# Two layer norms of a four-layer graph network without a mean: centred weights, a mean square on ScalarE, a mask on ScalarE, and new planner shares

## The chip, the cores and the metric

The kernel runs on one NeuronCore of a Trainium2 chip. The core has five engines with queues of their own, each of which works in order: TensorE (PE, with its weight loads as PEld), VectorE (DVE), ScalarE (ACT), GpSimd (POOL) and SyncE (SP, which only issues DMAs here). The metric is the time of one execution on the device, in microseconds (us), as the median of several runs; one further execution is profiled. Faster, the same and slower are relative to the kernel before.

## The reference

There are 32 graphs of 512 nodes with 64 features. Each graph has a sparse weighted adjacency matrix. Four layers follow each other, and each adds its result to its input and normalizes over the 64 features:

```python
def _layernorm(x, axis=-1, eps=1e-5):
    m = jnp.mean(x, axis=axis, keepdims=True)
    v = jnp.var(x, axis=axis, keepdims=True)
    return (x - m) / jnp.sqrt(v + eps)
...
    x = _layernorm(x + _L0_gnn_ref(x, adj), axis=-1)
    x = _layernorm(x + _L1_gnn_ref(x, adj, L1_gnn_weight, L1_gnn_bias), axis=-1)
    x = _layernorm(x + _L2_gnn_ref(x, adj, L2_gnn_att_W, L2_gnn_att_b), axis=-1)
    x = _layernorm(x + _L3_gnn_ref(x, adj, nodemask, L3_gnn_W1, L3_gnn_b1, L3_gnn_W2, L3_gnn_b2), axis=-1)
```

Layer 0 averages the neighbours. Layer 1 is a Chebyshev filter of four orders, whose results are multiplied by a weight of 256 x 64 and get a bias. Layer 2 is an attention in hyperbolic space over all pairs of nodes. Layer 3 takes weighted quantiles over each node's neighbours (which needs a sort) and feeds them through two dense products, `h = relu(out @ W1 + b1)`, `y = (h @ W2 + b2) * mask`. The norm after layer 1 and the norm after layer 3 are those that the change touches.

## The kernel before

Nodes lie on the 128 partitions, four tiles (T = 4) to a graph. Per graph the work is cut into lanes. *front* loads the adjacency matrix in four pieces, transposes it on PE, does layers 0 and 1 and normalizes into FL (lines 966 to 1054). *pairs* does the pairwise work of layer 2 in tiles of 128x512 and 128x640, and *tail* its end and norm (1056 to 1238). *graph* computes the neighbour lists and ranks (862 to 964). *gather* builds one-hot matrices and lets PE place the neighbours' features in slots (1240 to 1302). *sort* runs a sorting network on DVE over the tile SB, graph by graph, and *head* one over SH for two graphs together (1338 to 1393). *head* then calls `finish` and `dense` (1414 to 1459): ranked results go to DRAM, come back by an indirect DMA, and pass the two dense products, the mask, the residual add, the last norm and the output DMA. The last two graphs skip the way through DRAM (`spots`, the tiles "ends"). *check* tests limits; a dense fallback (1573 to 1709) is in the program but isn't taken with these inputs.

The order of the instructions is not the order of the code. The class `Order` (240 to 462) records every operation of all 32 graphs with its engine, an assumed cost and its dependencies. `due` (332) gives each a due time: the graph's number plus a share between the two numbers of its lane in `STAGES` (1506), times a period of 80. `issue` (357) then lets each engine take, of the operations that it assumes to be ready, the one due first. A handover between engines counts as the tail of the first operation plus `HOP` plus `LATE` (355). On PE, `STAY` (395) favours the weight shape in use. Where the plan leaves PE idle, small filler matmuls go in (`stay_active`, 1542 to 1545). The engines then run their queues in that fixed order and wait by semaphores.

A layer norm (796 to 811) is, on DVE, four `bn_stats` and four `bn_aggr` (one for each tile of nodes), an add of epsilon; on POOL a power of -0.5 (793); on DVE again the offset -mean times that; on ACT four activations with a scale and a bias for each node. It is called at 1008 (layer 0), 1047 (layer 1, which reads PE's result in PSUM), 1234 (layer 2) and 1458 (layer 3). In `front` the variance is used once more for the squared length of the normalized row (1051). The mask before the last norm is one DVE product of 128x256 (1456). `square` (826) and `scaled` (813) exist already and are used in the tail: four ACT squares that also give their sum, and four ACT copies with a scale for each node.

Of the kernel before, what the change touches and what calls it, by code (L numbers as in the profile page):

```python
# [15 lines left out]
OP = mybir.AluOpType  # L16
# [223 lines left out]
class Order:  # L240
# [3 lines left out]

    ENGINES = ("PE", "DVE", "ACT", "POOL", "SP")
    HOP = 0.05
    LATE = 0.124
    STAY = 39.7

    def __init__(self, nc, tc):  # L250
        self.nc, self.tc = nc, tc
# [214 lines left out]
def tile_adj_resnorm(ctx: ExitStack, tc: tile.TileContext, x, adj, nodemask, w1k, b1k, att_w, att_b,  # L466
# [221 lines left out]
    def rows(src, n, name, m, home=const):  # L688
        t = home.tile([m, n], F32, name=name)
        nc.scalar.dma_start(t, bass.AP(tensor=src.tensor, offset=src.offset, ap=[[0, m], [1, n]]))  # L690
        return t

    def parts3(src, name):

        rem, n = src, src.shape[-1]
        full = first.tile([3, n], F32, name=name + "s")
        part3 = first.tile([3, n], BF16, name=name + "p")
        out = const.tile([P, n], BF16, name=name)
        nc.vector.memset(out, 0.0)
        for k in range(3):  # L700
            nc.vector.tensor_copy(part3, rem)
            if k:
                stt(full, part3, identf[:3, k:k + 1], full, op0=OP.mult, op1=OP.add)
            else:
                ts(full, part3, identf[:3, 0:1], None, op0=OP.mult)
            tt(rem, rem, part3, op=OP.subtract)
        nc.vector.tensor_copy(out[:3, :], full)
        return out
# [1 line left out]
    b1f = first.tile([3, D + 2], F32, name="b1f")  # L710
    nc.scalar.dma_start(b1f[:, :D], bass.AP(tensor=b1k.tensor, offset=b1k.offset, ap=[[0, 3], [1, D]]))
    attb = rows(att_b, 1, "attb", P)
    bias2 = parts3(rows(b2, D, "b2f", 3, first), "bias2")
    meanf = first.tile([D, D], F32, name="meanf")
    nc.vector.memset(meanf, 1.0 / D)
    attw = const.tile([D, 2], F32, name="attw")
# [17 lines left out]
    nc.scalar.dma_start(b1s, b1.rearrange("(h u) -> h u", u=1))  # L734
    w2s = const.tile([HID, D], F32, name="w2s")
    nc.scalar.dma_start(w2s, w2)

    nmask = const.tile([P, T, B], F32, name="nmask")
    with tc.tile_pool(name="ps_0", bufs=1, space=PSUM) as ps:
        nm8 = first.tile([B, N], U8, name="nm8")  # L740
        nc.scalar.dma_start(nm8, nodemask)
        nmf = first.tile([B, N], F32, name="nmf")
        nc.vector.tensor_copy(nmf, nm8)
        pm = ps.tile([P, 512], F32, name="pm")
        for t in range(T):
            nc.tensor.transpose(pm[:, t * B:(t + 1) * B], nmf[:, t * P:(t + 1) * P], identf[:B, :B])
        nc.vector.tensor_copy(nmask, pm[:, :T * B].rearrange("p (t b) -> p t b", b=B))


        pw = ps.tile([P, 512], F32, name="pw")  # L750
        nc.tensor.matmul(pw[:D, :2], meanf, attw, start=True, stop=True)
        tt(attw, attw, pw[:D, :2], op=OP.subtract)
        wkT = first.tile([D, P], F32, name="wkT")
        for u in range(KO * D // P):
            pw = ps.tile([P, 512], F32, name="pw")
            nc.tensor.transpose(pw[:D, :P], wk[:, u, :D], identf)
            nc.vector.tensor_copy(wkT, pw[:D, :P])
            pw = ps.tile([P, 512], F32, name="pw")
            nc.tensor.matmul(pw[:, :2], wkT, attw, start=True, stop=True)
            nc.vector.tensor_copy(wk[:, u, D:], pw[:, :2])  # L760
        pw = ps.tile([P, 512], F32, name="pw")
        nc.tensor.matmul(pw[:3, :2], b1c.to_broadcast([D, 3]), attw, start=True, stop=True)
        nc.vector.tensor_copy(b1f[:, D:], pw[:3, :2])
    bias1 = parts3(b1f, "bias1")
    xs = dram.tile([B, N, D], F32, name="xs")
    ranked = [dram.tile([N, D], F32, name=f"ranked{b}") for b in range(B)]
# [7 lines left out]
    def bc(a, n=D):  # L774

        return a.unsqueeze(2).to_broadcast([P, T, n])
# [19 lines left out]
    def layernorm(dst, z):  # L796

        st = seq.tile(pools["small"], [P, T, nc.vector.BN_STATS_DIM], F32, "st", 2)
        mv = seq.tile(pools["small"], [P, T, nc.vector.BN_AGGR_DIM], F32, "mv", 2)
        for t in range(T):  # L800
            bn_stats(st[:, t, :], z[:, t, :])
        for t in range(T):
            bn_aggr(mv[:, t, :], st[:, t, :])
        var = col("var")
        ts(var, mv[:, :, 1], EPS, None, op0=OP.add)
        rs = rsqrt(var, "rs")
        off = col("off")
        stt(off, mv[:, :, 0], -1.0, rs, op0=OP.mult, op1=OP.mult)
        for t in range(T):
            act(dst[:, t, :], z[:, t, :], AF.Identity, bias=off[:, t:t + 1], scale=rs[:, t:t + 1])  # L810
        return mv[:, :, 1], rs

    def scaled(out, a, s):

# [151 lines left out]
    def front(b, res):  # L966

        A, xa = load(b)
        mid = pools["mid"]
        AT = transposed(A)  # L970
        res["AT"] = AT

        def amul(rhs, n):

            pt = bank()[:, :T * n].rearrange("p (t n) -> p t n", n=n)
            for t in range(T):
                for j in range(T):
                    mm(pt[:, t, :], AT[:, j, t * P:(t + 1) * P], rhs[:, j, :],
                                     start=(j == 0), stop=(j == T - 1))
            return pt  # L980

        def amul_split(y):

            half = N // 2
            pt = bank()[:, :half]
            for j in range(T):
                for h in range(2):
                    mm(pt[h * D:(h + 1) * D, :], y[:, j, :], AT[:, j, h * half:(h + 1) * half], start=(j == 0), stop=(j == T - 1),
                       pair=True)
            uT = seq.tile(mid, [P, half], F32, "uT", 1)  # L990
            act(uT, pt, AF.Copy)
            pt = bank()[:, :T * D]
            for u in range(2):
                tr(pt[:, u * P:(u + 1) * P], uT[:, u * P:(u + 1) * P], identf)
            return pt.rearrange("p (u h n) -> p h u n", h=2, n=D)


        pt = amul(xa, D + 1)
        deg = col("deg")
        cp(deg, pt[:, :, D])  # L1000
        dc = col("dc")
        ts(dc, deg, 1.0, None, op0=OP.max)
        recip(dc, dc)
        z = wide("z")
        tt(z, pt[:, :, :D], bc(dc), op=OP.mult)
        tt(z, z, xa[:, :, :D], op=OP.add)
        R = seq.tile(mid, [P, T, KO * D], F32, "R", 1)
        layernorm(R[:, :, :D], z)


        dm = col("dm")
        ts(dm, deg, 2e-35, None, op0=OP.max)
        dsc = rsqrt(dm, "dsc")
        pos = col("pos")
        ts(pos, deg, 0.0, None, op0=OP.is_gt)
        tt(dsc, dsc, pos, op=OP.mult)
        g = col("g")
        ts(g, deg, 0.0, None, op0=OP.not_equal)
        for k in range(1, KO):
            prev = R[:, :, (k - 1) * D:k * D]  # L1020
            y = wide("y")
            tt(y, prev, bc(dsc), op=OP.mult)
            pt = amul_split(y)
            q = wide("q", "y")
            tt(q.rearrange("p (h u) n -> p h u n", h=2), pt, dsc.rearrange("p (h u) -> p h u", h=2).unsqueeze(3).to_broadcast([P, 2, 2, D]),
               op=OP.mult)
            cur = R[:, :, k * D:(k + 1) * D]
            if k == 1:
                pg = wide("pg", "z")
                tt(pg, prev, bc(g), op=OP.mult)  # L1030
                prev = pg
            tt(cur, prev, q, op=OP.subtract)
        RT = seq.tile(mid, [P, KO * D // P, N], F32, "RT", 1)
        for u in range(KO * D // P):
            pt = bank()
            for t in range(T):
                tr(pt[:, t * P:(t + 1) * P], R[:, t, u * P:(u + 1) * P], identf)
            act(RT[:, u, :], pt, AF.Copy)
        pt = bank()[:, :T * (D + 2)].rearrange("p (t n) -> p t n", n=D + 2)
        nu = KO * D // P  # L1040
        for t in range(T):
            mm(pt[:, t, :], onesb, bias1, start=True, stop=False)
            for u in range(nu):
                mm(pt[:, t, :], RT[:, u, t * P:(t + 1) * P], wk[:, u, :], start=False, stop=(u == nu - 1))

        FL = FLS[:, b % 2]
        var, rs = layernorm(FL[:, :, :D], pt[:, :, :D])
        tt(FL[:, :, D + 2:D + 7:4], pt[:, :, D:], bc(rs, 2), op=OP.mult)

        w2 = col("w2")  # L1050
        stt(w2, var, float(D), rs, op0=OP.mult, op1=OP.mult)
        tt(FL[:, :, D:D + 34:33], bc(w2, 2), bc(rs, 2), op=OP.mult)
        ts(FL[:, :, D + 3:D + 36:32], bc(FL[:, :, D], 2), -1.0, 1.0, op0=OP.mult, op1=OP.add)
        res["FL"] = FL
# [381 lines left out]
    def dense(po, x3T, x3, dst, nm, home=None):  # L1436
# [16 lines left out]
            mm(py[:, t, :], onesb, bias2, start=True, stop=False)  # L1453
            mm(py[:, t, :], hT[:, t * P:(t + 1) * P], w2s, start=False, stop=True)
        z = home[1] if home else wide("zo")
        tt(z, py, bc(nm), op=OP.mult)
        tt(z, z, x3, op=OP.add)
        layernorm(z, z)
        dma(dst.rearrange("o (t p) d -> p (o t) d", p=P), z)

    flag = const.tile([1, 1], I32, name="flag")
# [13 lines left out]
    def within_bounds():  # L1475
# [17 lines left out]
        for i, op in enumerate((OP.is_gt, OP.is_lt)):  # L1493
# [9 lines left out]

    STAGES = {"front": (-0.6, -0.25), "pairs": (0.89, 1.46), "tail": (0.89, 1.49), "graph": (0.9, 1.59),
              "gather": (2.75, 2.76), "sort": (4.36, 5), "head": (4.74, 5.84), "ends": (2.6, 3.56), "check": (3.14, 3.68)}

    nc.scalar.preload_act_table_set("natural_log_exp_and_others")
    with ExitStack() as fast:  # L1510
# [285 lines left out]
```

## Time and profile before

| | before |
|---|---|
| timed runs, median of 3 | 2387.07 us (2385.55 to 2387.8) |
| profiled execution | 2391.38 us |
| its span, first to last instruction | 2389.5 us |
| granted PE clock, mean | 0.993 |
| PE fillers (lines 1544, 1545) | 761, busy 102.9 us |
| DVE group front_st<-front_bank (785) | 128, busy 29.1 us, mean 228 ns |
| DVE group head_st<-head_zo (785) | 124, busy 20.5 us, mean 209 ns |
| DVE group front_mv<-front_st (788) | 256, busy 33.8 us, mean 162 ns |
| DVE group head_zo<-head_bank,nmask (510) | 31, busy 12.8 us, mean 414 ns |
| ACT group tail_junk<-tail_u (546), and its accumulator reads | 128, busy 32.2 us, mean 252 ns; 128, busy 24.3 us, mean 190 ns |
| ACT group tail_v<-FLS,tail_s (546) | 128, busy 34.1 us, mean 337 ns |

Busy times of a group are the union of its instructions; neighbouring instructions of an engine overlap at their ends, so an instruction's duration is longer than the distance to the next one's start. A line number in a row may be that of a helper: 510 is a DVE operation on two tensors, 514 one with scalars, 517 one with a scalar and two tensors, 546 every ACT activation, 565 every matmul, 570 every transpose, 578 the indirect DMA, 793 the power on POOL. The prefix of a tile's name is its lane. "Idle before" is the time that the engine stood still just before an instruction, and after the arrow is what ended it.

### The profile page before, as it was taken

The numbers are of one execution on the slowest core, as the hardware profiler recorded it, in microseconds if no ns is written. First come the engines' busy times: TensorE is split into PE (matmuls) and PEld (weight loads), VectorE is DVE, ScalarE is ACT, GpSimd is POOL, SyncE is SP. The second block draws the span as 40 slices with busy tenths as digits, with TensorE's granted clock in tenths as the row PEclk, the third lists the DMA queues.
The fourth block names the chain that finished last, engine by engine and source line by source line (L and its number), as shares of the span: only waits on it lengthen the run. The fifth ranks groups of instructions, "written<-read, shape, count | busy, mean of one in ns | idle before, by whom it ended". The sixth has DMA issues, their size and how long they took to land.

```text
span 2389.5 us, 54114 instructions
## 1 busy us (share of the span) xinstructions
PE 2211.2 (93%) x19059; PEld 1559.4 (65%) x19059; DVE 2220.7 (93%) x7670; ACT 1862.6 (78%) x4602; POOL 1122.4 (47%) x2255
## 2 busy tenths in 40 slices
PE   7999999999999999999999999999999999999887
PEld 5666666666666666766666666666666666666555
DVE  4668899999999999999999999999999999999996
ACT  5788878787878877887887788787788878778841
POOL 1243345545454555545555544554545455454430
PEclk9999999999999999999999999999999999999999
DMA  1100001101001110100101010010101000000000
GB/s 42 34 28 23 15 15 31 27 23 35 19 19 27 28 29 24 32 17 23 28 27 31 23 32 17 23 28 26 32 23 32 16 25 26 21 21 4 15 15 11
DMA packets 131716, 57.75 MB, mean 24 GB/s; under 512 B 56140, under 2 KB 129516, under 8 KB 131436
## 3 DMA queue, kind: packets, MB, share of 16 engines
q1 hardware_dynamic: 126432, 50.09, 7.7%
q0 software_dynamic: 3840, 3.94, 0.9%
q8 instruction: 152, 2.49, 0.4%
q14 instruction: 128, 1.05, 0.1%
q10 hardware_dynamic: 1164, 0.18, 0.0%
HBM read 41.86 MB, written 12.32 MB: 23 GB/s over the span
## 4 chain that ended last, share of the span: by engine, by line
DVE 67%; PE 19%; ACT 7%; issue 4%; POOL 2%; DMA 0%; ACTq 0%; POOLq 0%; DVEq 0%
DVE SB L510 17%; PE front_bank L565 7%; DVE SH L510 7%; DVE gather_oh L514 7%; PE gather_bank L565 3%; DVE pairs_Wt L517 3%; PE graph_bank L565 3%; DVE pairs_L L517 3%; DVE pairs_Q L510 2%; PE pairs_bank L565 2%; DVE sort_prod L510 2%; DVE pairs_RW L510 2%; DVE pairs_EX L517 2%; DVE front_st L785 2%; DVE PRS L510 2%
## 5 line engine op out<-in xcount | busy, mean ns | idle before, releaser
L510 DVE TENSOR_TENSOR SB<-SB 128x92 f32<-128x92 f32 (+12 forms) x1312 | 548.3, 446 | 8.3
L565 PE MATMUL gather_bank<-gather_oh,tail_x3h 128*64 128x448 f16 (+5 forms) x5376 | 470.1, 317 | 2.8 <-ACT SB L546 2.3
L565 PEld LDWEIGHTS <-tail_x3h 128*64 128x64 bf16 x5376 | 293.2, 110 | 142.5 <-issue 43.0
L565 PE MATMUL pairs_bank<-pairs_FT 67*128 67x512 f32 (+7 forms) x768 | 309.9, 513 | 35.2 <-ACT pairs_FT L546 13.1
L510 DVE TENSOR_TENSOR SH<-SH 128x288 f32<-128x288 f32 (+18 forms) x880 | 269.2, 340 | 6.4
L514 DVE TENSOR_SCALAR gather_oh<-graph_slot 128x256 f16<-128x256 f16 (+9 forms) x864 | 257.0, 340 | 9.5 <-PE gather_bank L565 9.5
L565 PE MATMUL front_bank<-front_AT,front_y 128*64 128x256 f32 x1536 | 188.3, 383 | 23.7 <-DVE front_y L510 20.9
L565 PEld LDWEIGHTS pairs_bank<-pairs_FT 67*128 67x128 f32 (+1 forms) x768 | 127.5, 191 | 115.4 <-ACT pairs_EX L546 24.6
L578 POOL DMA_INDIRECT tail_x<-ranked,graph_spot x120 | 144.4, 1203 | 110.0 <-issue 68.9
L793 POOL TENSOR_TENSOR front_rs<-front_var,mhalf 128x4 f32<-128x4 f32 x64 | 91.4, 1428 | 204.2 <-DVE front_var L514 194.6
L565 PEld LDWEIGHTS front_bank<-front_AT,front_y 128*64 128x64 f32 x1536 | 118.5, 136 | 75.9 <-DVE front_y L510 29.2
L565 PEld LDWEIGHTS <-graph_nbT 128*128 128x128 f16 x1536 | 113.2, 97 | 62.0 <-issue 27.0
L565 PE MATMUL graph_bank<-graph_perm,graph_V 128*128 128x512 f16 x512 | 142.2, 379 | 7.3 <-ACT graph_VP L546 5.0
L565 PEld LDWEIGHTS pairs_bank<-FLS,pairs_Wt 128*128 128x128 f32 x1024 | 128.6, 191 | 22.4 <-DVE pairs_Wt L517 14.5
L565 PE MATMUL pairs_bank<-FLS,pairs_Wt 128*128 128x66 f32 x1024 | 130.7, 272 | 9.0 <-DVE pairs_Wt L517 7.3
L565 PEld LDWEIGHTS front_bank<-XA,front_AT 128*128 128x128 f32 x1024 | 127.8, 192 | 16.1 <-issue 6.3
L546 ACT ACTIVATE graph_V<-graph_bank 128x512 f16<-128x512 f32 x128 | 75.8, 592 | 74.4 <-PE graph_bank L565 74.3
L546 ACT ACTIVATE graph_slot<-graph_bank 128x512 f16<-128x512 f32 x128 | 75.6, 591 | 67.0 <-PE gather_bank L565 39.1
L565 PE MATMUL front_bank<-XA,front_AT 128*128 128x65 f32 x1024 | 124.3, 270 | 0.2 <-issue 0.2
L793 POOL TENSOR_TENSOR tail_rs<-tail_var,mhalf 128x4 f32<-128x4 f32 x32 | 40.0, 1251 | 162.0 <-DVE tail_var L514 86.3
L565 PEld LDWEIGHTS <-tabs 128*128 128x128 f16 x1296 | 78.3, 98 | 49.8 <-issue 32.0
L510 DVE TENSOR_TENSOR pairs_RW<-pairs_RW,pairs_EX 128x640 f32<-128x640 f32 x128 | 104.4, 816 | 6.7 <-ACT pairs_RW L546 6.7
(359 smaller groups left out, 6408.5 us busy)
## 6 DMA issues: line engine op xcount, KB each, us to landing
front_A<-in_adj_dram SPq DMA_DIRECT2D x128, 256.0 KB, 2.8
XA<-in_x_dram SPq DMA_DIRECT2D x32, 128.0 KB, 2.3
xs<-tail_x SPq DMA_DIRECT2D x32, 128.0 KB, 2.0
out_dram<-head_zo SPq DMA_DIRECT2D x31, 128.0 KB, 1.9
ranked<-sort_ap SPq DMA_DIRECT2D x30, 128.0 KB, 1.9
tail_x<-ranked,graph_spot POOLq DMA_INDIRECT x120, 2.5
out_dram<-tail_ends SPq DMA_DIRECT2D x1, 128.0 KB, 2.0
wk<-in_L_gnn_weight_dram ACTq DMA_DIRECT2D x1, 64.0 KB, 3.0
```

The costliest lines, as they stand in the source:

```text
L510: vec(lambda: nc.vector.tensor_tensor(out, a, b, op=op), out, [a, b])
L514: vec(lambda: nc.vector.tensor_scalar(out, a, s1, s2, op0=op0, **kw), out, [a], True, (s1, s2))
L517: vec(lambda: nc.vector.scalar_tensor_tensor(out, a, s, b, op0=op0, op1=op1), out, [a, b], False, (s,))
L546: 0.1, lambda: nc.scalar.activation(out, a, f, scale=scale, **kw), [out, accum_out], [a, after] + sc, table)
L565: return nc.tensor.matmul(out, w, a, start=start, stop=stop)
L578: seq.op("POOL", 1.15, 2.0, lambda: nc.gpsimd.indirect_dma_start(out, None, rows, bass.IndirectOffsetOnAxis(ap=at, axis=0)), [out], [at], ...
L785: vec(lambda: nc.vector.bn_stats(out, a), out, [a], reads=a)
L793: seq.op("POOL", 1.6, 0.5, lambda: nc.gpsimd.tensor_tensor(y, v, mhalf, op=OP.pow), [y], [v])
```

## The change

Subtracting from each row of a weight its mean over the 64 outputs makes every product of it have a mean of zero. For layer 1 the identity of the residual is already part of the weight (line 726), so the whole input of the norm is centred; the bias is centred too. For layer 3 the dense product is centred; the residual that is added to it is the output of the norm before, whose mean is zero, and the mask is one number for each node. So both norms leave out the mean: ACT takes the squares and their sum, DVE makes variance plus epsilon of it, POOL the power, ACT the product. The mask becomes four ACT copies with a scale. `LATE`, `STAY` and all of `STAGES` get new values.

```diff
-    LATE = 0.124
-    STAY = 39.7
+    LATE = 0.029
+    STAY = 31.6
...
+    def centred(a, n):
+
+        m = first.tile([a.shape[0], a.shape[1] if len(a.shape) > 2 else 1], F32, name=f"mean{n}")
+        for u in range(m.shape[1]):
+            row = a[:, u, :] if len(a.shape) > 2 else a
+            reduce(m[:, u:u + 1], row, OP.add)
+            ts(m[:, u:u + 1], m[:, u:u + 1], 1.0 / D, None, op0=OP.mult)
+            ts(row, row, m[:, u:u + 1], None, op0=OP.subtract)
+        return a
...
-    bias2 = parts3(rows(b2, D, "b2f", 3, first), "bias2")
+    bias2 = parts3(centred(rows(b2, D, "b2f", 3, first), 0), "bias2")
...
     nc.scalar.dma_start(w2s, w2)
+    centred(w2s, 1)
...
+    centred(wk[:, :, :D], 2)
+    centred(b1f[:, :D], 3)
     bias1 = parts3(b1f, "bias1")
...
+    def norm_centred(dst, z):
+
+        ss = square(z, "ss")
+        var = col("var")
+        ts(var, ss, 1.0 / D, EPS, op0=OP.mult, op1=OP.add)
+        rs = rsqrt(var, "rs")
+        scaled(dst, z, rs)
+        return ss, rs
...
-        var, rs = layernorm(FL[:, :, :D], pt[:, :, :D])
+        ss, rs = norm_centred(FL[:, :, :D], pt[:, :, :D])
...
-        stt(w2, var, float(D), rs, op0=OP.mult, op1=OP.mult)
+        tt(w2, ss, rs, op=OP.mult)
...
-        tt(z, py, bc(nm), op=OP.mult)
+        scaled(z, py, nm)
         tt(z, z, x3, op=OP.add)
-        layernorm(z, z)
+        norm_centred(z, z)
...
-    STAGES = {"front": (-0.6, -0.25), "pairs": (0.89, 1.46), "tail": (0.89, 1.49), "graph": (0.9, 1.59),
-              "gather": (2.75, 2.76), "sort": (4.36, 5), "head": (4.74, 5.84), "ends": (2.6, 3.56), "check": (3.14, 3.68)}
+    STAGES = {"front": (-0.46, -0.3), "pairs": (0.89, 1.21), "tail": (1.6, 2.5), "graph": (0.93, 1.24),
+              "gather": (2.63, 2.8), "sort": (3.87, 4.78), "head": (4.25, 5.37), "ends": (4.04, 4.45), "check": (1.75, 2.07)}
```

## The prediction

> **What bounds the kernel now.** I read the busy table first, then the same busy times cut into stretches of 280 us (four graphs), then the waits of VectorE (DVE), then the order of time on DVE and ScalarE (ACT).
>
> ```profile
> span 2389.5 us, 54114 instructions
> PE 2211.2 (93%) x19059; PEld 1559.4 (65%) x19059; DVE 2220.7 (93%) x7670; ACT 1862.6 (78%) x4602; POOL 1122.4 (47%) x2255
> ```
> ```profile
> core 0: us, PE busy (x) PEld busy (x) DVE busy (x) ACT busy (x) POOL busy (x), PEclk, DMA share, GB/s
> 760.00:1040.00 280.00, 262.94 (x2296) 185.96 (x2296) 273.79 (x946) 228.73 (x571) 143.87 (x275) 1.00 0.10 26
> 1040.00:1320.00 280.00, 262.95 (x2297) 185.91 (x2295) 273.77 (x946) 228.71 (x572) 143.85 (x275) 1.00 0.10 26
> 1320.00:1600.00 280.00, 262.95 (x2295) 185.84 (x2293) 273.80 (x945) 228.72 (x571) 143.89 (x275) 1.00 0.10 26
> ```
>
> The page gives PE and DVE 93% each and decides nothing. The stretches do: from about 140 us to 2360 us the work repeats (the same front matmul stands in the chain at 889.84, 1029.78 and 1169.71, so two graphs take 139.94 and one 69.97), and there DVE is busy 273.8 of 280, 97.8%. Per graph DVE is busy 68.45 and idle 1.55, PE 65.74 and 4.26, ACT 57.18 and 12.8. DVE sets the pace; the first 140 us (DVE busy 75.1) and the last 25 are ramps. The chain of waits agrees: DVE 67%, PE 19%.
>
> ```profile
> DVE front_st L785 <- PE front_bank L565: 16.0, 41, 0.8
> DVE pairs_RW L510 <- ACT pairs_RW L546: 4.1, 10, 0.4
> ```
>
> These are DVE's two largest waits between 480 and 1880 us, which is 20 graphs. Half of DVE's idle time (16.0/20 = 0.80 per graph) stands before the statistics of layer 1's last norm, which wait for one matmul group after the other.
>
> **What goes from DVE.** On a full queue an instruction costs the distance to the next one's start, less than its duration:
>
> ```profile
> 1043.58 0.41 DVE L510 TENSOR_TENSOR tail_v<-tail_v,tail_u 128x256 f32<-128x256 f32 x1
> 1043.92 0.34 DVE L514 TENSOR_SCALAR graph_v<-graph_v,graph_skip 128x512 f16<-128x512 f16 x1
> 1044.18 0.59 DVE L785 BATCH_NORM_STATS2 tail_st<-tail_v 128x6 f32<-128x64 f32 x4
> 1044.69 0.36 DVE L788 BATCH_NORM_AGGREGATE tail_mv<-tail_st 128x2 f32<-128x6 f32 x4
> 1044.97 0.32 DVE L514 TENSOR_SCALAR graph_v<-graph_v,graph_skip 128x512 f16<-128x512 f16 x1
> ...
> 1053.24 0.23 DVE L785 BATCH_NORM_STATS2 front_st<-front_bank 128x6 f32<-128x64 f32 x1
> 1053.39 0.21 DVE L514 TENSOR_SCALAR gather_oh<-graph_slot 128x256 f16<-128x256 f16 x1
> ```
>
> - Layer 1's norm: four statistics from PSUM at 0.15 (1053.24 to 1053.39), four aggregations at 0.10, the offset 0.07: 1.07. The new front_w costs 0.07 like the old.
> - The last norm: four statistics 0.51 (1044.18 to 1044.69), four aggregations 0.28, offset 0.07; the mask, 256 elements like tail_v, 0.34: 1.20.
>
> Together 2.27 per graph. The instruction order of the two programs, which I compared engine by engine, confirms the counts: 256 statistics, 256 aggregations, 64 offsets and 32 masks fewer, nothing added but 15 small instructions at the start. The other end of the price is the whole durations of the groups (29.1 + 16.9 + 4.9 and 21.1 + 11.4 + 4.8 + 13.2 = 101.4 us, 3.17 per graph); I take 2.27, because the queue is full, and keep 3.17 for the low end.
>
> **The wait of 0.80** moves to ACT, which now reads the front's bank group by group. DVE gets three new handovers per graph instead: front_var and head_var wait for ACT's sums, and the residual add for ACT's mask. Bounds: nothing, as tail_u shows (2.8 us in all after ACT's scaled copies, 0.09 per graph), to 0.4 each, the longest single pairs_RW wait, 1.2 per graph. I take 0.15 each, the size of the rows tail_v (4.6 us in all) and graph_v (4.5): 0.45.
>
> **What ACT gets.**
>
> ```profile
> 1078.13 1.06 ACT L546 ACTIVATE tail_v<-FLS,tail_s 128x64 f32<-128x64 f32 x4
> ```
>
> Squares with a sum already run in the tail: the tile's ACT busy time is 5.47 us in four graphs, 1.37 for four squares with their accumulator reads. Two such norms: 2.74. The mask as four scaled copies: 1.06 (the row above). The two last activations lose their bias operand and fall from 1.29 and about 1.45 to 1.06 each: -0.62. Net +3.18, so ACT goes from 57.2 to 60.4 in a step of about 67.4: 90%. What hides it is ACT's 12.8 us of idle time per graph, of which 2.4 is waiting for PE before graph_V; if that cover were gone, ACT would set a step of 69.97 + 3.18. PE's order before and after differs in fillers: 761 become 554, at 102.9/761 = 0.135 each 28 us of PE, all but 0.54 per graph of the old ones in the ramps.
>
> One rule speaks against the move of the mask: the Trainium skill, "ScalarE: Activation LUTs", section Rules for kernel authors, sends multiplications to VectorE. By its roughly 0.3 us per activation and 0.83 ns per element, four copies of 64 would be an estimated 1.4 us against the 1.06 in the row. The trace grants the rule that ACT's form is dearer (1.06 against 0.34), and on a kernel bound by ACT the sum by it would be a loss. Here the engine that is full is DVE, and the row decides.
>
> **Moved by the order.** The new shares (STAGES), LATE and STAY give other priorities, so all queues are reordered; the DMAs on SP and the work on POOL keep their counts. Pricing the DVE instructions of both orders with the rows above, between a graph's layer-1 work (front_pg) and its first sorted product lie 240 to 255 us in both, and the first sort stage comes after some 120 us in both: depth, ramp and drain stay, and I cost the new order at nothing, which only DVE's being fed in time covers. The old order repeats every two graphs; the new one doesn't, so I can't read its waits from a pattern. At the start, DVE's queue now has a reduction of w2s, whose DMA is issued at 7.58, ahead of identb; some 1.8 us of constants (7.69 to 9.50) move behind that landing, and the new instructions take about as much: +3 us (0 to 5). At the end ACT's masks and squares of the last two graphs replace shorter DVE work: +1.5 (0 to 3).
>
> **The sum.** 2.27 + 0.80 - 0.45 = 2.62 per graph, a step of 67.35. The first two graphs' fronts and the last two heads lie in ramps, so 30 graphs count: 78.6. Less 4.5 for start and end: 74. The profiled execution took 2391.4 (span 2389.5 and 1.9 around it) and lies 4.3 above the median of the timed runs, 2387.1. So 2391.4 - 74 = 2317, and **2313** as a median. Low end: 3.17 + 0.80 with no new wait, times 30, is 119; less nothing, 2268; I stop at 2275.
>
> **Rivals.**
>
> *PE takes over.* PE is busy 65.74 per graph. Without the old order's fillers 65.2; if it keeps its 4.26 of idle time, the step is 69.45, and 30 x 0.52 - 4.5 leaves 11: 2376. For it: front_y, front_q, uT and the single front bank make a serial loop that alternates PE, ACT and DVE. Against it: of PE's waits most are for DVE (front_y 6.5, front_st 5.2, pairs_L 2.9 us in the 560 us from 760), which shrink with DVE. The Trainium skill, "Perfetto Trace Analysis", section Identifying the Most-Contended Engine, calls the matmul row a bad measure and the weight-load share a better one. That share is 185.9 of 280, 66%; by the rule PE would be far from the bound and this rival dead, while by the busy row it is near. Chance 0.12, from 2345 to 2376.
>
> *Slower: handovers come late.* LATE, which the planner adds to every handover between engines, falls by 0.095 us. In the new order DVE's queue holds some 1,865 waits for PE, ACT and POOL, 58 per graph. If each came late by the margin removed, that is 5.5 per graph against the 3.07 gained: 30 x 2.4 + 4.5 gives 2465; at two thirds of it, 2409. It decides from 3.07/58 = 0.053 us per wait on. ACT, fuller by 3.18, is where lateness would begin. Against it:
>
> ```profile
> 1103.10 0.74 ACT L546 ACTIVATE pairs_RW<-pairs_RW 128x640 f32<-128x640 f32 x1
> ```
> ```profile
> 1103.87 0.82 DVE L510 TENSOR_TENSOR pairs_RW<-pairs_RW,pairs_EX 128x640 f32<-128x640 f32 x1 [0.40 <-ACT pairs_RW L546]
> ```
>
> ACT ends at 1103.84 and DVE, which waits for it, starts 0.03 later; the new planner still books 0.079 and a tail of 0.1. Chance 0.10. At its break-even point it gives no change: 0.05.
>
> **Chances.** Forecast (2275 to 2345) 0.73, PE 0.12, no change 0.05, slower 0.10. The range 2275 to 2376 leaves out the last two and a little below. Within 0.2% (4.8 us, about what this measurement can tell from no change) 0.05; faster 0.85; slower 0.10.
>
> **What would show it.** Right: DVE's busy share in the middle stretches stays at 96% or more while two graphs take near 134.7; front_st from the bank is gone from DVE's waits; ACT's share rises to about 90%; no ACT row leads DVE's waits. Wrong: DVE falls below 94% there, with waits for ACT's head_ss, front_ss or zo (slower rival), or PE rises over 96% with DVE waiting for front_bank (PE rival).

## The result and the profile after

The changed kernel took 2424.39 us (median of 4 runs, 2421.69 to 2432.62) beside 2387.44 for the kernel before (2385.55 to 2393.89): a ratio of 1.0156, 95% interval 1.0123 to 1.0188. It is slower by 1.6%; the forecast was 2313. The profiled execution took 2432.62 us with a span of 2430.8 and a mean granted clock of 0.971 (before: 0.993). In all ratios below, runs more than 1.5% above the fastest of their kernel are left out (a few single runs, and half of the ten of e9).

The busy table and the shares of the chain of waits, of the changed kernel:

```profile
PE 2249.2 (93%) x18852; PEld 1572.1 (65%) x18852; DVE 2158.2 (89%) x7077; ACT 1935.8 (80%) x5240; POOL 1065.8 (44%) x2255
```
```profile
DVE 48%; PE 22%; ACT 21%; POOL 5%; issue 4%; DMA 0%; ACTq 0%; POOLq 0%; DVEq 0%
```

VectorE lost its instructions as counted (593 fewer), and 62.5 us of busy time (2220.7 to 2158.2; 2.27 x 32 had made it 73). But its share of the chain fell from 67% to 48%, and ScalarE's rose from 7% to 21%: the chain that ended last now runs over ScalarE for a fifth of the span. The same stretches of 280 us as in the prediction:

```profile
core 0: us, PE busy (x) PEld busy (x) DVE busy (x) ACT busy (x) POOL busy (x), PEclk, DMA share, GB/s
760.00:1040.00 280.00, 264.84 (x2220) 187.27 (x2219) 258.83 (x848) 235.81 (x647) 134.08 (x266) 0.96 0.10 26
1040.00:1320.00 280.00, 261.01 (x2183) 181.73 (x2184) 255.16 (x820) 228.96 (x629) 128.11 (x262) 0.97 0.09 25
1320.00:1600.00 280.00, 260.21 (x2212) 183.54 (x2210) 258.59 (x841) 226.42 (x610) 129.65 (x268) 0.97 0.09 25
```

VectorE is busy 92%, not 96% or more; PE 93.6%; and the clock is 1.00 in none of the three. By VectorE's once-per-graph instruction front_pg, a graph takes 72.2 us on average between 480 and 1880 us (forecast 67.35, before 69.97). VectorE works 0.92 x 72.2 = 66.4 of these (forecast 68.45 - 2.27 = 66.2) and stands still 5.8 (forecast 1.2). Its waits in that window say for whom; the columns are us in total, times, longest:

```profile
DVE front_var L514 <- ACT front_junk L546: 27.2, 15, 3.3
DVE gather_oh L514 <- PE gather_bank L565: 12.1, 11, 2.4
DVE pairs_RW L510 <- ACT pairs_RW L546: 8.8, 8, 2.9
```

Summed over all rows of that view and per graph, VectorE waits 3.6 us for ScalarE (before 0.2) and 1.3 for PE (before 0.95). ScalarE waits 8.7 for PE (before 8.8). PE waits 3.2 for ScalarE (before 1.5) and 1.0 for VectorE (before 2.6), so in sum it stands still hardly longer than before: 87.4 us of these 1400 against 84.5. What grew are its stops of 0.35 us or more, from 79 (51 us in sum) to 115 (71 us). The new pair among the waits is this, two rows of the changed kernel:

```profile
ACT front_junk L546 <- PE front_bank L565: 42.8, 56, 3.0
```
```profile
PE front_bank L565 <- ACT front_junk L546: 22.2, 48, 0.7
```

PE waits for ScalarE's square and ScalarE's square for PE, on one bank (a bank is a piece of PSUM, where PE leaves its results). In order of time, first PE, then ScalarE, around 1066 us (start, duration, what, idle before it):

```profile
1064.84 0.64 PE L565 MATMUL front_bank<-wk,front_RT 128*128 128x66 f32 x4
1065.32 0.19 PE L565 MATMUL front_bank<-bias,onesb 128*128 128x66 bf16 x1
1066.11 0.66 PE L565 MATMUL front_bank<-wk,front_RT 128*128 128x66 f32 x4 [0.61 <-ACT front_junk L546]
...
1067.52 0.69 PE L565 MATMUL front_bank<-wk,front_RT 128*128 128x66 f32 x2 [0.47 <-ACT front_junk L546]
...
1069.17 0.31 PE L565 MATMUL graph_bank<-identb,graph_v 128*128 128x128 f16 x1
1069.28 0.31 PE L565 MATMUL graph_bank<-identb,graph_nbT 128*128 128x128 f16 x1
```
```profile
1065.87 0.19 ACT L546 ACTIVATION_READ_ACCUMULATOR front_junk<-front_bank 128x1 f32 x1
1065.96 0.43 ACT L546 ACTIVATE tail_x<-tail_v,tail_off,tail_rs 128x64 f32<-128x64 f32 x1
1067.15 0.22 ACT L546 ACTIVATE front_junk<-front_bank 128x64 f32<-128x64 f32 x1 [0.76 <-PE front_bank L565]
```

The four groups of layer 1 lie in one bank. PE stops in the third group until ScalarE has read the first, ScalarE then waits for PE, and so on: a turn on the bank costs what is ahead in ScalarE's queue too (here activations of tail_x). In the kernel before, VectorE read the bank in the same turns, but at once: PE's stops there were 0.3 us.

```profile
PE front_bank L565 <- DVE front_st L785: 12.9, 40, 0.3
```

The planner's dependencies go by region, not by bank, so it plans no such turn. Second, look at the last two PE rows above: small matmuls 0.11 us apart. The kernel before issues the same ones 0.055 apart:

```profile
1055.00 0.22 PE L565 MATMUL graph_bank<-identb,graph_v 128*128 128x128 f16 x1
1055.06 0.22 PE L565 MATMUL graph_bank<-identb,graph_nbT 128*128 128x128 f16 x1
```

In the changed kernel the granted clock was half from 1067.5 to 1070.9. Such stretches add up to 143 us in this trace (28 of them) and to 35 us before (6).

The Trainium skill, "PSUM — Partial Sum Buffer", section PSUM bank collisions raise a hardware error, says that two engines must not touch one bank in the same partitions at once, and that the compiler's scheduler adds a dependency between them whatever the addresses. The turns in both traces agree (48 stops of PE here, 40 before). The prediction did not weigh them when it gave the bank to a fuller engine.

### The profile page after: what moved, and what is told of

The parts are those of the page before. It is cut to its first block, busy times and chain, and to the rows that moved or that the text cites. A ratio compares the mean times of both kernels' runs of the same rounds, so it can differ in the third digit from the quotient of the medians.

```text
span 2430.8 us, 53659 instructions
## 1 busy us (share of the span) xinstructions
PE 2249.2 (93%) x18852; PEld 1572.1 (65%) x18852; DVE 2158.2 (89%) x7077; ACT 1935.8 (80%) x5240; POOL 1065.8 (44%) x2255
## 4 chain that ended last, share of the span: by engine, by line
DVE 48%; PE 22%; ACT 21%; POOL 5%; issue 4%; DMA 0%; ACTq 0%; POOLq 0%; DVEq 0%
DVE SB L510 12%; DVE SH L510 6%; PE front_bank L565 5%; PE gather_bank L565 4%; PE pairs_bank L565 4%; DVE gather_oh L514 4%; PE graph_bank L565 4%; DVE pairs_Wt L517 3%; DVE pairs_Q L510 2%; DVE sort_prod L510 2%; ACT pairs_RW L546 2%; DVE pairs_RW L510 2%; DVE pairs_L L517 2%; POOL tail_x L578 2%; DVE pairs_RW L517 1%
## 5 line engine op out<-in xcount | busy, mean ns | idle before, releaser
L510 DVE TENSOR_TENSOR SB<-SB 128x92 f32<-128x92 f32 (+12 forms) x1312 | 560.7, 447 | 12.9 <-ACT SB L546 5.3
L565 PE MATMUL gather_bank<-gather_oh,tail_x3h 128*64 128x448 f16 (+5 forms) x5376 | 491.3, 322 | 14.5 <-ACT SH L546 6.8
L565 PEld LDWEIGHTS <-tail_x3h 128*64 128x64 bf16 x5376 | 304.8, 112 | 159.0 <-issue 51.6
L565 PE MATMUL pairs_bank<-pairs_FT 67*128 67x512 f32 (+7 forms) x768 | 319.7, 523 | 16.3 <-ACT pairs_EX L546 10.3
L514 DVE TENSOR_SCALAR gather_oh<-graph_slot 128x256 f16<-128x256 f16 (+9 forms) x864 | 249.4, 341 | 27.1 <-PE gather_bank L565 26.7
L565 PEld LDWEIGHTS front_bank<-front_AT,front_y 128*64 128x64 f32 x1536 | 111.8, 140 | 92.4 <-DVE front_y L510 40.8
L578 POOL DMA_INDIRECT tail_x<-ranked,graph_spot x120 | 137.6, 1147 | 53.5 <-issue 38.5
L806 POOL TENSOR_TENSOR front_rs<-front_var,mhalf 128x4 f32<-128x4 f32 x64 | 83.2, 1300 | 173.3 <-DVE front_var L514 160.9
L510 DVE TENSOR_TENSOR pairs_RW<-pairs_RW,pairs_EX 128x640 f32<-128x640 f32 x128 | 104.6, 818 | 22.1 <-ACT pairs_RW L546 12.9
L546 ACT ACTIVATE SB<-gather_bank 128x448 f32<-128x448 f32 (+7 forms) x288 | 86.6, 349 | 46.3 <-PE gather_bank L565 41.4
L565 PE MATMUL front_bank<-wk,front_RT 128*128 128x66 f32 x512 | 85.6, 294 | 23.1 <-ACT front_junk L546 23.1
```

The source lines that it names most:

```text
L510: vec(lambda: nc.vector.tensor_tensor(out, a, b, op=op), out, [a, b])
L514: vec(lambda: nc.vector.tensor_scalar(out, a, s1, s2, op0=op0, **kw), out, [a], True, (s1, s2))
L546: 0.1, lambda: nc.scalar.activation(out, a, f, scale=scale, **kw), [out, accum_out], [a, after] + sc, table)
L565: return nc.tensor.matmul(out, w, a, start=start, stop=stop)
L578: seq.op("POOL", 1.15, 2.0, lambda: nc.gpsimd.indirect_dma_start(out, None, rows, bass.IndirectOffsetOnAxis(ap=at, axis=0)), [out], [at], ...
L806: seq.op("POOL", 1.6, 0.5, lambda: nc.gpsimd.tensor_tensor(y, v, mhalf, op=OP.pow), [y], [v])
```

## The experiments

Theories. **A**: the turns on layer 1's bank stop PE (and by that its clock), and ScalarE's lateness reaches VectorE. **B**: the new STAGES, LATE and STAY. **C**: the planner's low price of a square with a sum. **D** (the prediction): VectorE sets the pace and its saving is real. **P**: PE's loop takes over as soon as VectorE has room. **O**: the code is worth the forecast and only the new order spoils it.

Runs of one group below ran on one chip beside the kernel before; ratios are to it, with 95% intervals, as they stand on record (up to 0.4% off the quotient of the two medians). The first and third group met a chip on which the kernel before takes 2473 and 2467 us. Why is told at the end; it means that only kernels with the same order can be compared there.

### Parts of the change (kernel before: 2472.74)

The changed code with the old STAGES, LATE and STAY:

> The changed code with the old LATE, STAY and STAGES. Three theories. A (bank): PE and ACT take turns on the front's PSUM bank, square by square, and the stalls lower PE's clock; it lies in the code, so this stays slow, 2400 us or more, with PE waiting for front_junk as long as now (some 35 us) and over 100 us at half clock. B (shares): the smaller LATE and the new STAGES make a queue without slack; then this comes out near my forecast, 2313 us, and the clock is 0.99. C (price): the plan books a square with its sum at 0.20 to 0.24 us, the trace shows 0.37, ACT falls behind; it lies in the code, so this stays at 2400 or more too.

2397.76 us, 0.9718 (0.9680 to 0.9756).

The reverse, the code before with the new STAGES, LATE and STAY:

> The kernel before with the new LATE, STAY and STAGES alone, layer norms and mask as before. B (shares): slower than 2387, 2410 us or more, and the mean clock falls below 0.98. A (bank) and C (price): no square is added, so 2387 within 10 us.

2468.51 us, 0.9997 (0.9972 to 1.0023). Its order is another one than that of the kernel before, so on this chip it doesn't tell what the shares cost.

The changed kernel, with the squares from PSUM planned behind the bank's last matmul:

```diff
-        ss = square(z, "ss")
+        ss = square(z, "ss", z[:, T - 1, :] if z.space == PSUM else None)
...
-            act(..., AF.Square, accum_out=s[:, t:t + 1])
+            act(..., AF.Square, accum_out=s[:, t:t + 1], after=after)
```

> The changed kernel, but the plan puts the front's four squares behind the last matmul of their bank, so PE and ACT no longer take turns on it. A (bank): PE's wait for front_junk (35 us) and most of ACT's wait for front_bank before front_junk (62 us) go, and with them 30 us or more: 2395 or below. B and C: the waits go there, but the time stays within 10 us of 2424.

2405.43 us, 0.9731 (0.9697 to 0.9764). The changed kernel, with the planner's price of a sum at 0.2 in place of 0.09 us:

> The changed kernel, with one number of the plan changed: an accumulator output on ACT is booked at 0.20 instead of 0.09 us, which is what the trace shows for the pair of square and read. C (price): ACT no longer falls behind the plan, 2390 or below. A and B: another order, but the turns on the bank and the small margin stay, 2410 to 2435.

2463.58 us, 0.9964 (0.9940 to 0.9989). Without the changed kernel beside them these four don't give its parts. The truer price is 2.4% slower than e3 beside it and far from the 2390 that C gave, but the two orders differ, and on this chip that alone may do it. C was not run elsewhere and stays open.

### The changed kernel again (kernel before: 2399.28)

> The changed kernel unchanged, beside the kernel before, because the kernel before took 2387 us where the change was first measured and 2473 beside the first four experiments. If the change costs time wherever it runs, the ratio to the kernel before stays at 1.016. If what differs is how often TensorE's clock is granted in full to an order of work (half clock for 35 us in the kernel before and for 143 us in the changed one when first measured), the ratio may be anything, and follows the total of the half-clock stretches: with some 100 us of them in the kernel before, as its granted clock of 0.976 suggests, I expect the changed kernel 0 to 2% faster than it.

2427.58 us, 1.0111 (1.0094 to 1.0128): the loss is there again. The kernel before against itself:

> A copy of the kernel before: it gives the ratio of a kernel to itself (1.000 within 0.003) and a trace of the place where it is slow. If the clock is what makes it slow there, the trace has over 90 us of half clock (35 at first) and PE's busy time in the middle stretches rises with it, and DVE is busy less than 97.8% of them; if something else does (longer instructions on DVE, later DMAs), the half clock stays near 35 us and the rows of DVE or the DMAs are longer.

0.9988 (0.9971 to 1.0006); on this chip it isn't held up. e1 and e3 together, old shares and squares behind the bank's last matmul:

> The changed code with the old STAGES, LATE and STAY, and with the four squares of layer 1's norm planned behind the bank's last matmul. Theory A (turns on the bank stop PE, its clock falls): the old shares alone gave 0.972 of the kernel before, the squares behind the bank alone 0.973 of it; if both remove the same stops, this gives 0.970 to 0.975; if they remove different ones, 0.955 to 0.968. Theory B (the shares): the bank order is worth nothing with the old shares, 0.972 +- 0.004.

2397.07 us, 0.9999 (0.9979 to 1.0018). And the prediction's own slower rival, undone:

```diff
-    LATE = 0.029
+    LATE = 0.124
```

> The changed kernel with LATE at 0.124 again, its other new shares kept: every handover is planned 0.095 us later. My prediction's slower rival (handovers come late by the margin that LATE gave up): this takes the loss back, at least 20 us faster than the changed kernel beside it, and DVE's waits shrink. Theory A: LATE does not know of the turns on the bank, so the order is just another one, within 15 us of the changed kernel either way, and PE still waits for the front's squares.

2445.73 us, 1.0174 (1.0148 to 1.0200): 18 us slower than the changed kernel, not 20 us faster (and just outside the 15 us of theory A). VectorE's waits for ScalarE and PE don't shrink either: 91 us between 480 and 1880 us, in e5 89. Giving the margin back, with a new plan around it, doesn't take the loss back.

### The order of the kernel before, kept (kernel before: 2466.62)

Here the planner is shown the old instructions at their old prices, and only on issue each is replaced. PE, POOL and SP then get the queues of the kernel before, fillers included.

```diff
-            before[e] = self.pin(fn(), before.get(e))
+            for e, f in (fn if isinstance(fn, list) else [(e, fn)]):
+                before[e] = self.pin(f(), before.get(e))
...
+            vec([("ACT", lambda t=t, junk=junk: nc.scalar.activation(junk, z[:, t, :], AF.Square, accum_out=st[:, t, 0:1]))],
+                st[:, t, :], [z[:, t, :]], reads=z[:, t, :])
```

> The changed code in the order of the kernel before: the planner sees the old instructions at their old prices, and at the moment of issue each is replaced by the new one (a square on ScalarE where the statistic stood, nothing where the aggregation and the offset stood, four scaled copies where the mask stood). So every queue keeps its order, and fillers, waits for buffers and the pattern of two graphs stay. Theory O (the code is worth what I forecast and only the new plan spoils it): 2.3 to 3.1 us per graph, 0.960 to 0.975 of the kernel before on the same chip. Theory A (the new handovers between PE, ScalarE and VectorE cost what VectorE saves, whatever the order): 0.985 to 1.005, with VectorE's waits grown by 2 us per graph or more. Theory P (PE's serial loop sets the pace as soon as VectorE has room): 0.985 to 0.995, PE over 95% busy.

1.0039 (1.0003 to 1.0075); its ten runs spread from 2461 to 2523 us. PE is busy 91% between 200 and 2160 us, short of P's 95%. The same with nothing in exchange:

```diff
-            vec([("ACT", lambda t=t, junk=junk: ...AF.Square...)], st[:, t, :], [z[:, t, :]], reads=z[:, t, :])
+            vec([], st[:, t, :], [z[:, t, :]], reads=z[:, t, :])
...
-        vec(act4(z, py, nm), z, [py, bc(nm)])
-        tt(z, z, x3, op=OP.add)
+        vec([("DVE", lambda: nc.vector.tensor_tensor(z, py, x3, op=OP.add))], z, [py, bc(nm)])
+        vec([], z, [z, x3])
```

> What VectorE's saving is worth with nothing in exchange, in the order of the kernel before: the statistics, aggregations and offsets of both norms and the mask are left out and nothing replaces them (the variance is a constant computed from the bank, so the handover PE to VectorE to POOL stays; the output isn't the reference's). VectorE loses 2.34 us per graph by my rows. Theory D (VectorE sets the pace, as the prediction says): 0.960 to 0.973. Theory P (PE's serial loop is as near as that): 0.985 or more, PE over 95% busy in the middle stretches and VectorE's waits for PE grown by what it lost.

2391.83 us, 0.9718 (0.9664 to 0.9771). Layer 1's norm alone, then the last norm and the mask alone:

> Layer 1's norm alone in the order of the kernel before (four squares on ScalarE from the bank, where PE's next group waits for the square). Theory A: this is the half that costs: 1.000 or more, with PE's waits for the front's squares of 0.5 us per graph or more. Theories O and D: 1.07 + 0.80 us per graph saved less handovers, 0.978 to 0.990.

> The last norm and the mask alone in the order of the kernel before. Nothing of it meets PE's loop but the mask's read of the bank. Theories A, O and D agree on 1.20 us per graph less handovers: 0.984 to 0.992. Theory P: 0.993 or more. If ScalarE's queue is too full at that place: over 1.000 with VectorE's wait for the masked tile over 1 us per graph.

2469.69 us, 0.9998 (0.9963 to 1.0032), and 2502.67 us, 1.0120 (1.0073 to 1.0166). So O falls: in the old order, too, what VectorE is spared (2.8%) is gone once ScalarE does it instead. Each half of the change has its wait, over the whole run of e11 and of e12 (32 graphs):

```profile
DVE front_var L843 <- ACT front_junk L838: 61.4, 31, 4.1
```
```profile
DVE head_var L843 <- ACT head_junk L838: 40.6, 31, 1.8
...
DVE head_zo L512 <- ACT head_zo L830: 18.4, 16, 10.4
```

61.4/32 = 1.9 us per graph for layer 1's sums, against 1.07 + 0.80 to be gained there. 40.6/32 = 1.3 for the last norm's sums alone, against 1.20. A, O and D had expected e12 to be faster; only the condition at the end of its expectation (ScalarE too full at that place) came near, and there it is the sums, more than the masked tile, that come late (10.4 of head_zo's 18.4 us are one wait at the very end of the run). PE's stops for layer 1's reader are little longer in e11 (25.3 us over the run) than in e12, where VectorE still reads the bank (21.3): in a kept order it is ScalarE's lateness that costs.

This chip holds ScalarE up for 5.6 us in about every second graph (told at the end), so look at the graphs between. There front_var waits 1.71 us in e11, and the old statistics in e12 wait 0.72, as in the kernel before on the first chip: 0.99 more, against 1.07 of work saved. From one front_pg to the next, the distances without such a stop alternate between 72.3 and 67.6 us in the kernel before on the first chip. In e10 they are 70.4 and 65.0, in e9 72.2 and 72.6, in e12 72.3 and 71.6 (the 72.6 and the 71.6 occur once each). So it is not this chip alone that eats the saving.

### What the changed kernel's loss consists of (kernel before: 2390.49)

> The changed kernel unchanged, as the base for the three kernels beside it: the first four experiments ran where the kernel before took 2473 us, without the changed kernel beside them. Where the kernel before takes 2387 to 2400 us I expect 2420 to 2430 again; where it takes 2470, the changed kernel's order has other matmuls behind the fetched rows and I expect 2425 to 2460.

2433.51 us, 1.0141 (1.0083 to 1.0200). The same program has now been profiled three times, with 127, 143 and 168 us of half clock (e5, the first run, e13). Beside it, fillers in PE's waits, found in its trace and put ahead of the matmul that waits:

```diff
+                for _ in range(self.WARM.get(count, 0)):
+                    before[e] = self.pin(filler(), before.get(e))
+                count += 1
                 spare = t + ops[i][1]
```

> The changed kernel in its own order on every engine, with 496 short filler matmuls put ahead of the 148 matmuls for which PE waited 0.35 us or more in its trace (100 to 2300 us), as many as the wait holds. No instruction is moved and no wait is removed; only PE's idle time is filled. If the half clock (143 us of it in the changed kernel) is a cause of its own, the half-clock total falls under 50 us and the time by 15 to 60 us. If the half clock is only the mark of PE's waits, the time stays within 8 us or grows, whether the clock rises or not.

2398.73 us, 1.0025 (0.9999 to 1.0051), 35 us under e13. Half clock fell from 168 us to 44. The third stretch of e13 and of e14:

```profile
1040.00:1320.00 280.00, 261.38 (x2179) 182.16 (x2178) 252.63 (x811) 226.43 (x615) 126.10 (x264) 0.96 0.09 25
```
```profile
1040.00:1320.00 280.00, 269.00 (x2325) 187.13 (x2329) 260.66 (x856) 234.08 (x646) 129.53 (x270) 1.00 0.10 26
```

The traces of e13 and e14 have the same instructions in the same order on VectorE and on ScalarE, and VectorE gets 8 us more work done in 280. So the half clock is a cause of its own: 124 us less of it, 35 us. The 25 runs of the kernel before beside them agree: worked out from their granted clocks (twice the missing share, times the span), they had 14 to 67 us of half clock, and each us more goes with 0.43 us of time. The bank and the shares, beside the same base:

> The changed kernel with the four squares of layer 1's norm planned behind the bank's last matmul, now beside the changed kernel. Theory A (turns on the bank): 15 to 30 us faster than it. If it is within 8 us of it, the turns are not worth what their waits add up to.

> The changed code under the old STAGES, LATE and STAY, now beside the changed kernel. Theory B (the new shares are the cause): at least 25 us faster than the changed kernel and faster than the kernel before by 1% or more where that takes 2387 to 2400. Theory A: the shares bring 10 to 30 us, and the time stays at or above the kernel before there.

e15: 2387.23 us, 0.9958 (0.9931 to 0.9986), 46 us under e13. Between 480 and 1880 us PE no longer waits for front_junk, VectorE's front_var does for 0.2 us in all, and half clock falls to 89 us; PE's longest sum of waits is now

```profile
PE front_bank L565 <- DVE front_y L510: 10.6, 25, 1.5
```

e16: 2392.01 us, 0.9994 (0.9963 to 1.0025), 41 us under e13, with 90 us of half clock. B holds in part: the old shares avoid as much, but they don't bring the forecast; the kernel is where it was before the change. Its turns on the bank, which A had expected to be as long as before (e1), are shorter, but not gone:

```profile
PE front_bank L565 <- ACT front_junk L546: 13.7, 32, 0.5
```

e7 takes these away as well (no such row is left in its trace), and is no better than e16 for it: 0.9999 against 0.9994, on another chip. And e15 and e16 both plan every engine's queue anew, unlike e14. So what the turns cost by themselves isn't shown: under the new shares at most e15's 46 us, of which its new order may be a part, and under the old shares nothing that can be seen.

### The ceiling, and a version faster than both (kernel before: 2397.33)

Both remedies together, e15 with fillers in the waits that are left in its trace:

> The kernel of e15 (squares planned behind the bank's last matmul) with 453 fillers put ahead of the 118 matmuls for which PE waited 0.35 us or more in its trace. It has 89 us of half clock left. In e14 123 us of half clock less gave 35 us; at that rate 50 to 60 us less give 15 us: 2372 where the kernel before takes 2390, a ratio of 0.990 to 0.994, faster than both. If the two remedies act on the same stops, it stays at 0.994 to 0.998.

2363.85 us (2362.8 to 2366.66), 0.9866 (0.9841 to 0.9891): 1.3% faster than the kernel before, and better than expected. Half clock is down to 22 us. And e10 on a chip where the kernel before isn't held up:

> The kernel of e10 (both norms' statistics, aggregations and offsets and the mask left out, nothing put in their place, order of the kernel before; the output isn't the reference's) beside a kernel before that takes 2390, if the chip allows. If VectorE sets the pace there, 2.34 us per graph are 70 us: 0.968 to 0.974, and VectorE stays over 96% busy in the middle stretches. If PE's stops take over, 0.980 or more, and VectorE falls under 95%.

2309.78 us, 0.9640 (0.9615 to 0.9664). The first stretch and VectorE's waits between 480 and 1880 us:

```profile
760.00:1040.00 280.00, 268.62 (x2401) 193.69 (x2400) 275.42 (x899) 234.02 (x596) 149.05 (x286) 1.00 0.10 27
```
```profile
DVE gather_oh L516 <- PE gather_bank L567: 4.8, 10, 0.5
DVE pairs_RW L512 <- ACT pairs_RW L548: 4.5, 11, 0.4
```

VectorE is busy 98.4%, and a graph takes 67.45 us. D holds and P falls: without an exchange VectorE keeps the pace and the saving arrives whole, even a little over the expected 0.968. PE is busy 96% there, so little room is left behind VectorE. The wait ahead of layer 1's norm has gone, too. What separates e17 from it (54 us, 1.7 per graph) fits the exchange that is left: VectorE waits 1.6 us per graph for ScalarE and 1.15 for PE in e17, 0.2 and 0.2 in e18.

## Why the prediction was wrong, by its steps

- **VectorE bounds the kernel; 2.27 us per graph go.** Right, the price a little high (2.05 measured: 68.45 to 66.4). e18 leaves out nearly the same work and gives 67.45 per graph. That this is so near the predicted step of 67.35 is partly luck: e18 has none of the new waits of 0.45, and by the prediction's own terms it would be 69.97 - 2.34 - 0.80 = 66.83.
- **"The wait of 0.80 moves to ACT."** This failed. The wait was one half of a turn on a bank, and the other half is PE's. With a reader whose queue is fuller, both halves grew: between 480 and 1880 us PE's stops for the reader went from 12.9 to 22.2 us, and the reader's waits there from VectorE's 16.0 to ScalarE's 42.8. e15, planned without the turns, is 46 us faster; how much of that is the turns is open (e7).
- **New waits of 0.45, bounds 0 to 1.2.** Too small. This is the term of the sum that failed most plainly: front_var alone is 27.2 us in 19.4 graphs, 1.40 each, against 0.15 taken and 0.4 as its upper end. The bound came from rows where VectorE waits for a ScalarE that is itself supplied (pairs_RW, 0.4); a safer one would have come from rows where ScalarE itself waits for PE (graph_V in the kernel before: 49.8 us, longest 4.1).
- **"What hides it is ACT's 12.8 us of idle time per graph."** This failed. ScalarE's work was right (0.823 x 72.2 = 59.4 us per graph, forecast 60.4), but 8.8 of the idle 12.8 was waiting for PE already. Idle time that lies in waits is no room for work that somebody needs at once: VectorE's waits for ScalarE rose by 3.4 us per graph, more than the 3.07 to be gained.
- **The new order costed at nothing.** This failed. It was said to rest on VectorE being fed in time, and VectorE wasn't. The order set under the new shares is 41 us dearer for the same code (e13, e16), and between 480 and 1880 us it has 1 filler where the kernel before has 70, which the prediction counted as 0.54 us per graph of PE time saved; e14 put fillers back and was faster.
- **A term that is missing: the clock.** The profile before showed PEclk 1.00, and the prediction took it as given. Under PE's new pattern of stops it fell to half for 143 us (before 35); e14 prices 124 us of half clock at 35 us. The Trainium skill, "TensorE: Matmul & The Clock Gate", Part 1, has the clock fall to 4/8 after an idle window of about 3.4 us. Here PE wasn't idle in the 3.4 us ahead of these stretches: its records show it busy for 21 to 80% of them, half of the time for about two thirds or more. The measurement decides: ahead of 12 of the 28 stretches no stop was longer than 0.47 us.
- **The rivals.** The slower one held the measured time (2409 to 2465), and it named ScalarE as the place where lateness begins. But its mechanism, LATE's margin, is not borne out by e8. With 0.10 it had too small a chance, since its place was right whatever the margin; that its number came out is luck. PE did not take over (e18).

So two things are shown. The exchange by itself pays nothing: with ScalarE doing the work, the code is at the time of the kernel before under the old shares (e16) and no faster in the kept order (e9). And the new order costs some 41 us more. The pieces overlap and can't be added: e14's 35, e15's 46 and e16's 41 us each bring the changed kernel back to about the kernel before, and e15 and e16 have about half of e13's half clock.

## What to carry to other kernels

Work taken from the engine that sets the pace pays in full only if whoever gets it can answer at once: look not at the receiver's idle time but at what it is waiting for in it. When the reader of a PSUM bank changes, count PE's stops on that bank as well, and read the granted clock as a price of PE's stops, not as a given. Before a saving is believed, leave the work out with the order kept: that gives the ceiling, and the rest is the exchange.

## What was not expected of the hardware

The half clock comes without an idle window, and filling PE's stops with short matmuls gives the full clock back (168 to 44 us of half clock, 35 us of time). In the changed kernel's trace all 28 stretches of half clock start on one grid of 3.413 us. Of the windows of this grid between 100 and 2300 us that ran at the full clock, all 6 in which PE's records show it busy under 60% were followed by half clock, 10 of 19 with 60 to 70%, 8 of 37 with 70 to 80%, and none of 547 with more. In e13, the same program, 2 of 91 with 80 to 90% were, and again none with more than 90%. So there is no sharp threshold in these traces; only the fullest windows were always safe.

On one of the four chips that the experiments met, the kernel before takes 2467 to 2473 us instead of 2387 to 2399, while e16's kernel takes 2398 there and 2392 elsewhere. In the kept order PE's transposes of the rows that an indirect DMA brings back stand early in its queue. First and third transpose, in e6 and then in e11 on that chip:

```profile
832.74 0.27 PE L570 MATMUL head_bank<-identf,tail_x 128*128 128x128 f32 x1
...
836.14 0.28 PE L570 MATMUL head_bank<-identf,tail_x 128*128 128x128 f32 x1
```
```profile
845.81 0.27 PE L572 MATMUL head_bank<-identf,tail_x 128*128 128x128 f32 x1
...
854.91 0.42 PE L572 MATMUL head_bank<-identf,tail_x 128*128 128x128 f32 x1
```

The third comes 3.4 us after the first in one and 9.1 in the other. In between, front_q on VectorE and front_RT on ScalarE wait for something whose origin the trace of e11 doesn't name (21.8 and 67.3 us over the run, in 12 stops each). That the rows land later on that chip is argued from this; their landings aren't in that trace.
